# Graph attention on one core: layer 2 with row tiles for five units instead of nine, and a unit's work in another order

## The chip, the cores and the metric

The kernel runs on one core of one Trainium2 chip. Its time is the device time of one execution in microseconds, the median over several runs. The engines are PE (TensorE, matmuls and transposes; its weight loads are listed as PEld), DVE (VectorE), ACT (ScalarE), POOL (GpSimd) and SP (SyncE, which here only issues DMAs). All data are float32 unless said otherwise.

## What is computed

The input is x (8 batches, 2048 nodes, 64 features) and one adjacency matrix of 2048 x 2048 zeros and ones, which all batches share. The densest nodes come first: the chance of a link falls with both node numbers. Cut to what matters:

```python
def _gat_layer(h, mask, b):
    scores = einsum('...nd,...md->...nm', h, h)
    attn = softmax(where(mask, scores, -1e16))
    return einsum('...nm,...md->...nd', attn, h) + b

mask = adj + eye(2048) > 0
h    = einsum('bnc,hdc->bhnd', x, Wh)                  # 4 heads of 64
z    = leaky_relu(cat of _gat_layer(h, mask, bh), 0.2) # layer 1
h2   = einsum('bnk,dk->bnd', z, Wo)                    # 256 -> 64
z2   = leaky_relu(_gat_layer(h2, mask, bo), 0.2)       # layer 2
out  = layernorm(x + layernorm(z2) * gamma + beta)
```

## The kernel before, in words

**Sets and lists.** The first 56 nodes (HUB) have many neighbours and are done densely. The other 1992 are cut into NS = 166 sets of 12. For each set the kernel finds, on the chip, a list of at most 128 nodes that hold all neighbours of the twelve (one column of `index`), and works only with those. One *gather* (`gather`, L797) fetches the rows of such a list: an indirect DMA that POOL issues, 128 rows of 2080 bytes (520 floats: four pairs of batches, each with two columns of ones for the sums), into a *row tile* of 128 partitions.

**Layer 1** works on 83 groups of two sets. Its end writes the rows of the second layer's table (`table2`, L902, issued by SP and at the last by ACT). Near its end the tiles of the first eight blocks of hub work are loaded into the layer-1 row tiles.

**Layer 2** is the place of the change. Its 166 sets make NU = 42 units of four (the last has two). A unit u passes through these steps:
- four gathers into four row tiles (POOL),
- `turn2(u)`: each row tile is transposed by PE in four 128 x 128 pieces (L513), and ACT copies the result out of PSUM into `xts` (L1368; two tiles by one copy of 128 x 1024),
- `scores2(u)`: 32 matmuls of 128 x 128 into the PSUM bank `bank[0]` (L1223), and the exponential by ACT into `eT` (L1226),
- `turn_scores(u)`: four transposes back into the same bank (L1234),
- `keep_scores(u)`: DVE multiplies with the mask `linked` and keeps the weights in `es2` (L1242),
- `values2(u)`: 64 matmuls with the row tiles (L1253), two units into one PSUM tile,
- after every second unit the division by the sums, activation, two layernorms and the residual (`norm`, DVE and ACT), spread over the following units by `work_on(u, 0)` and `work_on(u, 1)`; `roots` (L1326, L1327) takes reciprocal roots on ACT, SP stores the output,
- `spread_own(u)` (L1033, ACT) lays out a unit's own columns, which scores2 needs as weights.

The hub nodes' own attention runs beside this in 19 blocks: `hub_step(k)` makes the scores of block k (L1070, eight matmuls; L1079 DVE, L1082 ACT) and the values of block k-1 (L1093, 16 matmuls). Steps 3 to 8 stand right ahead of layer 2's loop, with scores in `bank[0]`; steps 9 to 19 stand in it, two in the round of u = -3 and one in each after that. Their row tiles `hrows` (six, loaded by SP, `hub_block`, L1059) are filled for blocks 8 to 13 at the start of layer 2 and again inside the loop.

**The order.** Each engine runs its own instructions in the order of the program, and waits on semaphores; nothing reorders them. The loop runs u from -3 and issues, in each round: `turn2(u+3)`, `scores2(u+2)`, a hub step, `values2(u)`, the gathers of unit u+9, `work_on(u, 0)`, `spread_own(u+3)`, `turn_scores(u+1)`, `keep_scores(u+1)`, `work_on(u, 1)`, `roots(u)`. There are 36 row tiles, so the gathers of units 0 to 8 are all issued at the start of layer 2 without a wait between them, and unit u+9 takes the tiles of unit u, each gather waiting for the matmuls of values2 that read its tile. The tiles lie in SBUF in the order of their allocation: first the 36 row tiles, then `xts`, then `hrows`, all in space that layer 1 has used, and what lay there decides what a first write waits for.

Of the kernel before, what the change touches and what calls it, by code (L numbers as in the profile page):

```python
# [30 lines left out]
F32 = mybir.dt.float32  # L31
# [5 lines left out]
OP = mybir.AluOpType  # L37
# [322 lines left out]
def fast_kernel(ctx: ExitStack, tc: tile.TileContext, x, adj, Wh, bh, Wo, bo, gamma, beta, out, flag):  # L360


    nc = tc.nc
    B, N, C = x.shape
# [145 lines left out]
    def turn(tp, rows):  # L510

        for q in range(Q):
            nc.tensor.transpose(tp[:, q * P:(q + 1) * P], rows[:, q, 1:1 + P], ident)  # L513
# [276 lines left out]

    rows = {}
    held = {}

    def gather(table, s, layer, new):
        t = rows[layer, s] = new(f"g{layer}_{s}")
        bound = {} if layer == 2 and s < 36 else dict(bounds_check=N - 1, oob_is_err=False)
        nc.gpsimd.indirect_dma_start(out=t.rearrange("n q c -> n (q c)"), out_offset=None, in_=table,  # L797
                                     in_offset=bass.IndirectOffsetOnAxis(ap=index[:, s:s + 1], axis=0), **bound)

# [253 lines left out]
    def hub_block(k, t):  # L1053
        b = hub_order[k]
        rows["h", k] = t
        n = HUB if b == NHB else hub_sets(b)[1] * SET
        s0 = b * S10
        src = table2[:HUB, :] if b == NHB else table2[HUB:, :].rearrange("(k s) c -> s k c", s=NS)[s0:s0 + n // SET]
        nc.sync.dma_start(out=t.rearrange("n q c -> n (q c)")[:n], in_=src)  # L1059
# [145 lines left out]
    def rows2(name):  # L1205
        return rowt2[int(name[3:]) % 36]

    xts = [late.tile([P, 2, 512], F32, name=f"xts{k}", bufs=1) for k in range(4)]
    hrows = [late.tile([P, Q, PW], F32, name=f"hrows{k}", bufs=1) for k in range(6)]
    for k in range(6):  # L1210
        hub_block(8 + k, hrows[k])
    for u in range(9):
        for s in sets[u]:
            gather(table2, s, 2, rows2)

    def scores2(u):

        w = len(sets[u])
        sp = bank[0].rearrange("p (k n) -> p k n", k=4)
        for k, s in enumerate(sets[u]):  # L1220
            xt = held["T", 2, s // 2].rearrange("c j (q n) -> c j q n", q=Q)
            for q in range(Q):
                nc.tensor.matmul(sp[q * 32:(q + 1) * 32, k, :], bd[u % 3][:, k, q, :], xt[:, s % 2, q, :], start=True, stop=True,  # L1223
                                 tile_position=(0, q * 32))
        e = held["E", u] = late.tile([P, 4, P], F32, tag="eT", name=f"eT{u}", bufs=2)
        nc.scalar.activation(e[:, :w], sp[:, :w], AF.Exp, bias=shifts[:, 1:2], scale=1.0)  # L1226
# [125 lines left out]
    def spread(u, parts):  # L1352

        for k, part in enumerate(parts):
            for t in range(2):
                jobs.setdefault((u + k, t), []).extend(part[t])

    def work_on(u, t):
        for job in jobs.pop((u, t), ()):
            job()  # L1360

    def turn2(u):
        for g in sorted({s // 2 for s in sets[u]}):
# [4 lines left out]
            nc.scalar.copy(t, tp)  # L1368

    tot = late.tile([P, 8], F32, name="tot", bufs=1)  # L1370

# [13 lines left out]
    def in_limits():  # L1385

        nc.vector.tensor_reduce(tot[:, 5:6], tot[:, 0:5], AX.X, OP.min)
        pf = bank2("pf", "T", 2)
        nc.tensor.matmul(pf[0:1, 0, 0:1], tot[:, 5:6], ones, start=True, stop=True)
        fl = late.tile([1, 1], I32, name="fl", bufs=1)  # L1390
        nc.vector.tensor_scalar(fl, pf[0:1, 0, 0:1], P - 0.5, None, OP.is_lt)
        nc.sync.dma_start(out=flag, in_=fl)

    k = 9
    for u in range(-3, NU + 5):
        if u + 3 < NU:
            turn2(u + 3)
        if 0 <= u + 2 < NU:
            scores2(u + 2)
        for _ in range(2 if u == -3 else 1):  # L1400
            if k <= NHB + 1:
                hub_step(k, bank2(f"sh{k}", "T", 2)[:, 0, :] if k <= NHB else None)
                if 8 <= k - 1 and k + 5 <= NHB:
                    hub_block(k + 5, hrows[(k - 1 - 8) % 6])
                if k == NHB + 1:
                    spread(u + 2 - u % 2, norm_hub(u + 2 - u % 2, oh2))
                k += 1
# [9 lines left out]
        work_on(u, 0)  # L1417
        if 3 <= u + 3 < NU:
            spread_own(u + 3)
        if 0 <= u + 1 < NU:  # L1420
            turn_scores(u + 1)
            a = (u + 1) % 2
# [3 lines left out]
            keep_scores(u + 1, a)  # L1426
        work_on(u, 1)
        roots(u)
# [46 lines left out]
```

## Time and profile before

| | |
|---|---|
| time, median of 3 runs | 1018.35 us (1017.01 to 1022.75) |
| span of the profiled execution | 1021.0 us |
| PE busy | 807.8 us (79%) |
| DVE busy | 617.2 us (60%) |
| ACT busy | 521.4 us (51%) |
| POOL busy | 481.3 us (47%) |
| gathers of layer 2, L797 | 166, 1024 ns each, 170.0 us |
| transposes of layer 2, L513 | 664, 280 ns each, 91.6 us |

The profiled execution is one run; its span is 2.65 us above the median. In the page's picture by slices the span is cut into 40 equal parts, and each digit is the busy share of one in tenths. In a timeline a row has its start, its length, engine, line, operation, tiles written and read, the count, and in brackets how long the engine was idle before it and what ended that; "issue" there means that nothing which the profile shows was waited for. Matmuls are pipelined, and their ends are modelled. In the rows by window a window's length is followed by each engine's busy time and count, the granted clock of PE, the share of DMA time and the rate in GB/s.

### The profile page before, as it was taken

The page shows a single profiled execution, that of the slowest core. Times are in us where ns is not written, and L with a number is a line of the kernel's source. Part 1 is how long each engine was busy: PE and PEld are TensorE (multiplying, and loading weights), DVE is VectorE, ACT ScalarE, POOL GpSimd, SP SyncE. Part 2 cuts the span into 40 slices and gives each one's busy share as a digit, 9 for nine tenths or more (in the row PEclk, how much of TensorE's full clock was granted, in tenths as well). Part 3 has the DMA queues.
Part 4 walks back from the last instruction along what each step waited for, and adds up shares of the span by engine and source line. Part 5 has one row for each costly group of instructions (what it writes and reads, how often), then busy time and mean ns, then how long its engine had stood idle before and what let it go on. Part 6 is the DMA issues. An engine that isn't in the chain of part 4 may idle for free.

```text
span 1021.0 us, 42671 instructions
## 1 busy us (share of the span) xinstructions
PE 807.8 (79%) x18437; PEld 685.5 (67%) x18437; DVE 617.2 (60%) x1376; ACT 521.4 (51%) x1042; POOL 481.3 (47%) x614
## 2 busy tenths in 40 slices
PE   3976679899999999999999998419786676667760
PEld 2644457788898888888888887307665555555750
DVE  3449844678777777745555555002267766766795
ACT  2423335556566666666666665005445645555651
POOL 6533214474454555556556630750456556655100
PEclk9989989999999999999999999658999999999985
DMA  8876412453233344444444432764345555445221
GB/s 184 238 208 171 118 44 59 131 134 80 75 91 83 103 124 123 120 124 115 120 119 113 120 86 75 193 184 128 91 112 141 152 147 142 125 134 138 76 53 29
DMA packets 81790, 122.52 MB, mean 120 GB/s; under 512 B 35568, under 2 KB 51852, under 8 KB 81594
## 3 DMA queue, kind: packets, MB, share of 16 engines
q0 software_dynamic: 26784, 65.84, 24.9%
q1 hardware_dynamic: 37702, 49.57, 16.3%
q10 hardware_dynamic: 17108, 4.30, 2.3%
q8 instruction: 147, 2.41, 1.0%
q14 instruction: 49, 0.40, 0.1%
HBM read 123.91 MB, written 18.48 MB: 139 GB/s over the span
## 4 chain that ended last, share of the span: by engine, by line
PE 56%; DVE 13%; issue 9%; ACT 8%; another core or an unknown queue 6%; DMA 4%; POOL 2%; SPq 1%; DVEq 0%; POOLq 0%; ACTq 0%
PE s L826 10%; PE o L851 8%; PE bank L513 7%; PE t L513 6%; PE cat L811 5%; ACT xts L1368 3%; DMA raw<-in_adj_dram 3%; PE cat L532 3%; PE o L868 3%; PE cat L885 3%; PE bank L1234 2%; PE bank L1223 2%; PE cat L895 2%; PE o L1253 2%
## 5 line engine op out<-in xcount | busy, mean ns | idle before, releaser
L797 POOL DMA_INDIRECT g<-table,index x166 | 176.6, 1064 | 207.2 <-PE o L851 165.7
L797 POOL DMA_INDIRECT rows<-table,index x166 | 170.0, 1024 | 147.3 <-PE o L1253 87.5
L831 DVE TENSOR_TENSOR e<-s,mask 128x768 f32<-128x768 f32 x83 | 79.4, 957 | 95.2 <-PE s L826 94.8
L826 PE MATMUL s<-y,xTg 64*64 64x48 f32 x5312 | 115.4, 222 | 5.4 <-issue 3.5
L513 PE MATMUL t<-ident,rows 128*128 128x128 f32 x664 | 91.6, 280 | 31.8 <-issue 30.4
L826 PEld LDWEIGHTS s<-y,xTg 64*64 64x64 f32 x5312 | 98.9, 134 | 25.6 <-issue 20.2
L1368 ACT COPY xts<-t 128x1024 f32<-128x1024 f32 x83 | 79.9, 1011 | 56.2 <-PE t L513 48.5
L513 PEld LDWEIGHTS t<-ident,rows 128*128 128x128 f32 x664 | 76.3, 144 | 40.9 <-issue 39.8
L513 PE MATMUL bank<-ident,g 128*128 128x128 f32 x664 | 100.2, 274 | 0.2 <-ACT otbh L634 0.2
L851 PE MATMUL o<-g,e 128*64 128x65 f32 x2656 | 98.0, 226 | 2.4 <-issue 2.4
L519 ACT ACTIVATE z<-cat,bhp 128x192 f32<-128x192 f32 x166 | 60.7, 417 | 73.9 <-PE cat L532 70.8
L851 PEld LDWEIGHTS o<-g,e 128*64 128x64 f32 x2656 | 85.8, 138 | 12.8 <-issue 3.0
L1129 ACT COPY xTg<-bank 128x512 f32<-128x512 f32 x166 | 89.1, 596 | 0.5 <-PE bank L513 0.3
L1223 PE MATMUL bank<-xts,share 128*32 128x128 f32 x1328 | 56.2, 278 | 34.4 <-issue 19.7
L513 PEld LDWEIGHTS bank<-ident,g 128*128 128x128 f32 x664 | 79.9, 142 | 2.8 <-DVE keysi L766 0.6
L838 ACT ACTIVATE e<-e,shifts 128x768 f32<-128x768 f32 x83 | 80.0, 964 | 2.5 <-DVE e L831 2.5
L817 ACT COPY y<-cat 128x384 f32<-128x384 f32 (+1 forms) x80 | 40.7, 509 | 68.5 <-DVE rowt L899 37.3
L598 ACT ACTIVATE e<-e,shifts 128x896 f32<-128x896 f32 x32 | 33.4, 1043 | 81.4 <-DVE e L595 65.6
L1223 PEld LDWEIGHTS bank<-xts,share 128*32 128x32 f32 x1328 | 38.1, 109 | 50.9 <-issue 44.2
L681 POOL TENSOR_SCALAR a<-raw 120x1024 bf16<-120x1024 int32 (+1 forms) x34 | 38.5, 1135 | 62.1 <-DMA raw<-in_adj_dram 34.7
L811 PE MATMUL cat<-xo,gram 128*128 128x192 f32 (+1 forms) x320 | 65.0, 326 | 0.0
L858 DVE RECIPROCAL rall<-o 64x8 f32<-64x8 f32 x166 | 34.1, 205 | 50.5 <-PE o L851 49.1
(190 smaller groups left out, 1563.0 us busy)
## 6 DMA issues: line engine op xcount, KB each, us to landing
raw<-in_adj_dram SPq DMA_DIRECT2D x32, 480.0 KB
table<-xb SPq DMA_DIRECT2D x22, 256.0 KB
xr_s<-table SPq DMA_DIRECT2D x21, 256.0 KB
table<-x SPq DMA_DIRECT2D x16, 260.0 KB
x<-in_x_dram ACTq DMA_DIRECT2D x32, 128.0 KB
table<-rowt SPq DMA_DIRECT2D x164, 24.4 KB
xb<-in_x_dram SPq DMA_DIRECT2D x164, 24.0 KB
out_dram<-y_s SPq DMA_DIRECT2D x162, 24.0 KB
```

The costliest lines, as they stand in the source:

```text
L513: nc.tensor.transpose(tp[:, q * P:(q + 1) * P], rows[:, q, 1:1 + P], ident)
L519: nc.scalar.activation(z[:, hp], cat[:, :, hp * n:(hp + 1) * n], AF.Identity, bias=bhp[:, hp:hp + 1], scale=1.0)
L797: nc.gpsimd.indirect_dma_start(out=t.rearrange("n q c -> n (q c)"), out_offset=None, in_=table, in_offset=bass.IndirectOffsetOnAxis(ap=ind ...
L811: nc.tensor.matmul(cat[:, k, 2 * GM:2 * GM + n], gram[:, g % 2 * 2 + k, :], held["x", g // 2][:, :n], start=True, stop=True)
L817: nc.scalar.copy(held["y", g // 2][:, :n, g % 2 * 2:g % 2 * 2 + 2], cat[:, :, 2 * GM:2 * GM + n].rearrange("p a n -> p n a"))
L826: nc.tensor.matmul(sp[half(r), p, (q * 2 + j) * M:(q * 2 + j + 1) * M], xt[half(p), j, q, half(r)], y[half(p), (j * Q + q) * M:(j * Q + q ...
L831: nc.vector.tensor_tensor(e[:, :16 * M].rearrange("p (a q n) -> p a q n", a=2, q=Q), sp[:, :, :8 * M].rearrange("p a (q n) -> p a q n", q= ...
L838: nc.scalar.activation(e[:, :16 * M], e[:, :16 * M], AF.Exp, bias=shifts[:, 0:1], scale=1.0)
L851: nc.tensor.matmul(op[half(p), j, o0:o0 + K1], e[:, c0:c0 + 64], rw[j][:, q, sums(p)], start=True, stop=True)
L1129: nc.scalar.copy(t[:, k, :], bank[k])
L1223: nc.tensor.matmul(sp[q * 32:(q + 1) * 32, k, :], bd[u % 3][:, k, q, :], xt[:, s % 2, q, :], start=True, stop=True, tile_position=(0, q * 32))
L1368: nc.scalar.copy(t, tp)
```

## The change

Line numbers behind the change grow by 2 to 9: L797 becomes L799, L1059 L1061, L1223 L1232, L1234 L1243, L1242 L1251, L1253 L1262, L1368 L1377. Five things are different in layer 2; layer 1 is as before.

1. The ring has 20 row tiles (units in flight, LEAD, 5) instead of 36. At the start only the gathers of units 0 and 1 are issued. Those of units 2, 3 and 4 follow in the rounds of u = -3, -2 and -1, each behind a copy of one element on POOL (`seen`) that reads the last tile turned in that round. From u = 0 on, unit u+5 takes the tiles of unit u after values2(u).
2. The four gathers of a unit are issued with the last set first.
3. `xts` and `hrows` are allocated ahead of the row tiles, so they lie elsewhere.
4. A round has another order: values2(u), the gathers of unit u+5, turn_scores(u+1), work_on(u, 0), keep_scores(u+1), a hub step, turn2(u+3), (for u < 0: `seen` and the gathers), scores2(u+2), work_on(u, 1), spread_own(u+3), roots(u).
5. turn2 takes one PSUM bank for each set, with four in flight, and ACT copies 128 x 512 four times a unit instead of 128 x 1024 twice.

```diff
+    LEAD = 5
+    RING = 4 * LEAD
...
-        bound = {} if layer == 2 and s < 36 else dict(bounds_check=N - 1, oob_is_err=False)
+        bound = {} if layer == 2 and s < RING else dict(bounds_check=N - 1, oob_is_err=False)
...
-        nc.vector.tensor_scalar(index[:, :36], index[:, :36], N - 1, None, OP.bitwise_and)
+        nc.vector.tensor_scalar(index[:, :RING], index[:, :RING], N - 1, None, OP.bitwise_and)
...
-    rowt2 = [late.tile([P, Q, PW], F32, name=f"rows2_{k}", bufs=1) for k in range(36)]
...
     xts = [late.tile([P, 2, 512], F32, name=f"xts{k}", bufs=1) for k in range(4)]
     hrows = [late.tile([P, Q, PW], F32, name=f"hrows{k}", bufs=1) for k in range(6)]
+    rowt2 = [late.tile([P, Q, PW], F32, name=f"rows2_{k}", bufs=1) for k in range(RING)]
+    seen = late.tile([1, 1], F32, name="seen", bufs=1)
...
+    def gathers(u):
+        for s in sets[u][-1:] + sets[u][:-1]:
+            gather(table2, s, 2, rows2)
+
     for k in range(6):
         hub_block(8 + k, hrows[k])
-    for u in range(9):
-        for s in sets[u]:
-            gather(table2, s, 2, rows2)
+    for u in range(2):
+        gathers(u)
...
     def turn2(u):
-        for g in sorted({s // 2 for s in sets[u]}):
-            tp = bank2(f"t2_{g}", "T", 2)
-            for j in range(2):
-                turn(tp[:, j, :], rows[2, 2 * g + j])
-            t = held["T", 2, g] = xts[g % 4]
-            nc.scalar.copy(t, tp)
+        for s in sets[u]:
+            if s % 2 == 0:
+                held["T", 2, s // 2] = xts[s // 2 % 4]
+            tp = bank1(f"t2_{s}")
+            turn(tp, rows[2, s])
+            nc.scalar.copy(xts[s // 2 % 4][:, s % 2, :], tp)
...
     for u in range(-3, NU + 5):
-        if u + 3 < NU:
-            turn2(u + 3)
-        if 0 <= u + 2 < NU:
-            scores2(u + 2)
-        for _ in range(2 if u == -3 else 1):
...
             values2(op, sets[u], es2[a], a, len(sets[u + 1]) if a == 0 else 0)
             if a == 1:
                 spread(u, norm_sets(u // 2, op))
-        for s in sets[u + 9] if 0 <= u < NU - 9 else []:
-            gather(table2, s, 2, rows2)
+            if u + LEAD < NU:
+                gathers(u + LEAD)
+        if 0 <= u + 1 < NU:
+            turn_scores(u + 1)
         work_on(u, 0)
+        if 0 <= u + 1 < NU:
...
+            keep_scores(u + 1, a)
+        for _ in range(2 if u == -3 else 1):
...
+        if u + 3 < NU:
+            turn2(u + 3)
+        if u < 0:
+            nc.gpsimd.tensor_copy(seen, held["T", 2, sets[u + 3][-1] // 2][0:1, 1, 0:1])
+            gathers(u + LEAD)
+        if 0 <= u + 2 < NU:
+            scores2(u + 2)
+        work_on(u, 1)
         if 3 <= u + 3 < NU:
             spread_own(u + 3)
```

What that does to the engines is shown at three places. The rows give line, operation, the tile written, the tiles read, and in brackets the semaphores waited for, by the engine or DMA queue that signals them; `rows_k` is a row tile, `table` the table of layer 2. First POOL at the start of layer 2, before: the first gathers of the 36.

```order
L797 DMA rows_0_11559<-table_99,index 128x520 [waits DMAHW3_49,DMAHW4_49,DMAHW2_49,DMAHW5_49,DMAHW1_49,DMAHW6_49,DMAHW0_49,DMAHW7_49,DMASW3_49,PE_49]
L797 DMA rows_1_11560<-table_99,index 128x520 [waits DVE_49,DMASW4_49,Activation_49,Pool_49]
L797 DMA rows_2_11561<-table_99,index 128x520 [waits DMASW5_49]
L797 DMA rows_3_11562<-table_99,index 128x520 [waits DMASW6_49]
L797 DMA rows_4_11563<-table_99,index 128x520 [waits DMASW7_49]
L797 DMA rows_5_11564<-table_99,index 128x520 [waits DMASW0_49]
```

The same place now, from the seventh gather on:

```order
L799 DMA rows_5_11574<-table_99,index 128x520 [waits DMASW1_49]
L799 DMA rows_6_11575<-table_99,index 128x520 [waits DMASW2_49]
L1434 COPY seen<-xts_11560 1x1 [waits Activation_49]
L799 DMA rows_11_11580<-table_99,index 128x520 [waits DMASW3_49]
L799 DMA rows_8_11577<-table_99,index 128x520 [waits DMASW4_49]
L799 DMA rows_9_11578<-table_99,index 128x520 [waits DMASW5_49]
L799 DMA rows_10_11579<-table_99,index 128x520 [waits DMASW6_49]
L1434 COPY seen<-xts_11562 1x1 [waits Activation_49,Pool_49]
```

After eight gathers stands a copy that waits for ACT, then four gathers, then the next copy; before, none of the following ones waited for a compute engine.

The second place is POOL in the loop, before: unit 9 takes the tiles of unit 0, unit 10 those of unit 1.

```order
L797 DMA rows_0_11559<-table_99,index 128x520 [waits DMASW7_49,PE_49]
L797 DMA rows_1_11560<-table_99,index 128x520 [waits DMASW0_49,PE_49]
L797 DMA rows_2_11561<-table_99,index 128x520 [waits DMASW1_49,PE_49]
L797 DMA rows_3_11562<-table_99,index 128x520 [waits DMASW2_49,PE_49]
L797 DMA rows_4_11563<-table_99,index 128x520 [waits DMASW3_49,PE_49]
```

And now, unit 5 in the tiles of unit 0 and unit 6 in those of unit 1:

```order
L799 DMA rows_3_11572<-table_99,index 128x520 [waits DMASW7_49,PE_49]
L799 DMA rows_0_11569<-table_99,index 128x520 [waits DMASW0_49]
L799 DMA rows_1_11570<-table_99,index 128x520 [waits DMASW1_49]
L799 DMA rows_2_11571<-table_99,index 128x520 [waits DMASW2_49]
L799 DMA rows_7_11576<-table_99,index 128x520 [waits DMASW3_49,PE_49]
```

Each of four gathers waited for PE; now the first does, for the last set of values2, and the other three only for their DMA lane.

The third place is SP at the start of layer 2, before: the last store into the table of layer 2, and the loads of hub tiles.

```order
L902 DMA table_99<-rowt_114 4x12x130 [waits DMAHW0_49,DVE_49]
L1059 DMA hrows_11599<-table_99 120x1x520 [waits DMAHW5_49,DMAHW1_49,PE_49]
L1059 DMA hrows_11600<-table_99 120x1x520 [waits DMAHW2_49]
L1059 DMA hrows_11601<-table_99 120x1x520 [waits DMAHW3_49]
L1059 DMA hrows_11602<-table_99 120x1x520 [waits DMAHW4_49]
```

And now:

```order
L904 DMA table_99<-rowt_114 4x12x130 [waits DMAHW0_49,DVE_49]
L1061 DMA hrows_11563<-table_99 120x1x520 [waits DMAHW1_49,Activation_49,Pool_49]
L1061 DMA hrows_11564<-table_99 120x1x520 [waits DMAHW2_49]
L1061 DMA hrows_11565<-table_99 120x1x520 [waits DMAHW3_49]
L1061 DMA hrows_11566<-table_99 120x1x520 [waits DMAHW4_49]
```

The first load waited for PE, namely for the hub values of block 7 (L1093), which read a tile that lay in the same space; now it waits for ACT and POOL, for work that belongs to layer 1, and not for PE.

More of the change, by code (lines that the diff above doesn't have):

```diff
@@ L1201, in bank2, with bank1, rows2 @@
         return psum2.tile([P, 2, 512], F32, tag=tag, name=name, bufs=bufs)
-    rowt2 = [late.tile([P, Q, PW], F32, name=f"rows2_{k}", bufs=1) for k in range(36)]
-    def rows2(name):
-        return rowt2[int(name[3:]) % 36]
     xts = [late.tile([P, 2, 512], F32, name=f"xts{k}", bufs=1) for k in range(4)]
     hrows = [late.tile([P, Q, PW], F32, name=f"hrows{k}", bufs=1) for k in range(6)]
+    rowt2 = [late.tile([P, Q, PW], F32, name=f"rows2_{k}", bufs=1) for k in range(RING)]
+    seen = late.tile([1, 1], F32, name="seen", bufs=1)
+    def bank1(name):
+        return psum2.tile([P, 512], F32, tag="T", name=name, bufs=4)
+    def rows2(name):
+        return rowt2[int(name[3:]) % RING]
+    def gathers(u):
+        for s in sets[u][-1:] + sets[u][:-1]:
+            gather(table2, s, 2, rows2)
     for k in range(6):
         hub_block(8 + k, hrows[k])
-    for u in range(9):
-        for s in sets[u]:
-            gather(table2, s, 2, rows2)
+    for u in range(2):
+        gathers(u)
     def scores2(u):
@@ L1387, in in_limits @@
         nc.vector.tensor_reduce(tot[:, 5:6], tot[:, 0:5], AX.X, OP.min)
-        pf = bank2("pf", "T", 2)
-        nc.tensor.matmul(pf[0:1, 0, 0:1], tot[:, 5:6], ones, start=True, stop=True)
+        pf = bank1("pf")
+        nc.tensor.matmul(pf[0:1, 0:1], tot[:, 5:6], ones, start=True, stop=True)
         fl = late.tile([1, 1], I32, name="fl", bufs=1)
-        nc.vector.tensor_scalar(fl, pf[0:1, 0, 0:1], P - 0.5, None, OP.is_lt)
+        nc.vector.tensor_scalar(fl, pf[0:1, 0:1], P - 0.5, None, OP.is_lt)
         nc.sync.dma_start(out=flag, in_=fl)
@@ L1395, in fast_kernel @@
     for u in range(-3, NU + 5):
-        if u + 3 < NU:
-            turn2(u + 3)
-        if 0 <= u + 2 < NU:
-            scores2(u + 2)
-        for _ in range(2 if u == -3 else 1):
[L1401 to L1407, printed above, removed]
         if 0 <= u < NU:
@@ L1414, in fast_kernel @@
                 spread(u, norm_sets(u // 2, op))
-        for s in sets[u + 9] if 0 <= u < NU - 9 else []:
-            gather(table2, s, 2, rows2)
-        work_on(u, 0)
-        if 3 <= u + 3 < NU:
-            spread_own(u + 3)
+            if u + LEAD < NU:
+                gathers(u + LEAD)
         if 0 <= u + 1 < NU:
             turn_scores(u + 1)
+        work_on(u, 0)
+        if 0 <= u + 1 < NU:
             a = (u + 1) % 2
@@ L1426, in fast_kernel @@
             keep_scores(u + 1, a)
+        for _ in range(2 if u == -3 else 1):
+            if k <= NHB + 1:
+                hub_step(k, bank1(f"sh{k}") if k <= NHB else None)
+                if 8 <= k - 1 and k + 5 <= NHB:
+                    hub_block(k + 5, hrows[(k - 1 - 8) % 6])
+                if k == NHB + 1:
+                    spread(u + 2 - u % 2, norm_hub(u + 2 - u % 2, oh2))
+                k += 1
+        if u + 3 < NU:
[5 more added lines that the diff above has]
+            scores2(u + 2)
         work_on(u, 1)
+        if 3 <= u + 3 < NU:
+            spread_own(u + 3)
         roots(u)
```

## The prediction

> **What bounds the kernel now.** I read the page first, then the chain of waits between 620 and 730 us, the timeline around its longest piece, SP's waits, and last the windows and groups of layer 2. The page says that no engine is full over the whole span, and that PE collapses in the middle of it:
>
> ```profile
> span 1021.0 us, 42671 instructions
> PE   3976679899999999999999998419786676667760
> POOL 6533214474454555556556630750456556655100
> ```
>
> A digit is 25.5 us. PE's 26th and 27th are 4 and 1, at 638 to 689 us, where POOL's are 7 and 5: here layer 2 begins. The chain of waits shows what the end of the kernel hangs on there:
>
> ```profile
> 636.05 53.60 another core or an unknown queue
> 689.65 3.67 DMA hrows<-table
> 693.46 1.14 PE bank L1093 x16
> ...
> 697.53 2.25 PE t L513 x16
> 699.78 1.01 PE bank L1223 x32
> ...
> 702.43 1.90 PE t L513 x16
> ...
> 711.96 1.04 PE o L1253 x64
> ...
> 720.57 1.04 PE o L1253 x64
> ```
>
> The chain has no name for 53.60 us. SP's waits have the same length at the load of a hub tile, which suits one wait on PE, and the timeline shows what POOL and PE do meanwhile:
>
> ```profile
> SPq L1059 <- remote: 53.8, 1, 53.8
> ```
>
> ```profile
> 638.71 0.98 POOL L797 DMA_INDIRECT rows<-table,index  x1 [4.47 <-ACT share L1082]
> 639.99 0.96 POOL L797 DMA_INDIRECT rows<-table,index  x1 [0.30 <-issue]
> ...
> 641.94 1.09 PE L1070 MATMUL bank<-share,own 128*120 128x112 f32 x8 [0.72 <-issue]
> ...
> 648.12 1.94 PE L1070 MATMUL bank<-share,own 128*120 128x112 f32 x8 [4.48 <-DVE share L1079]
> ...
> 682.52 0.95 POOL L797 DMA_INDIRECT rows<-table,index  x1 [0.30 <-issue]
> ...
> 687.42 0.37 PE L513 MATMUL t<-ident,rows 128*128 128x128 f32 x1 [1.03 <-issue]
> ```
>
> ```profile
> 660.00:680.00 20.00, 3.18 (x9) 1.65 (x9) 0.00 (x0) 0.00 (x0) 15.13 (x16) 0.50 0.75 211
> ```
>
> POOL issues 36 gathers back to back (638.71 to 682.52: 1.25 us each). PE runs nine transposes in 20 us, waiting for nothing but "issue", DVE and ACT run nothing. The gate opens when the gathers stop: 16 transposes that trickled until 687.42 take 2.25 us at 697.53. So a train of gathers holds PE, and the hub load (which waits for PE to have read an older tile) comes after it.
>
> The units behind this, cut at the starts of values2 of units 0, 6, 32, 36 and 41 and the end (time, PE, PEld, DVE, ACT, POOL, clock, DMA):
>
> ```profile
> 711.90:764.30 52.40, 41.39 (x804) 33.47 (x802) 21.18 (x40) 23.18 (x40) 24.91 (x24) 0.93 0.37 97
> 764.30:948.10 183.80, 128.57 (x3018) 107.49 (x3021) 125.47 (x223) 103.26 (x189) 108.71 (x104) 1.00 0.52 140
> 948.10:971.50 23.40, 19.25 (x472) 17.58 (x475) 18.94 (x34) 16.55 (x30) 2.25 (x2) 0.93 0.26 65
> 971.50:993.90 22.40, 14.68 (x454) 12.82 (x442) 20.64 (x39) 11.34 (x24) 0.00 (x0) 0.88 0.21 50
> 993.90:1021.00 27.10, 1.28 (x34) 0.94 (x34) 15.69 (x31) 3.88 (x10) 1.20 (x2) 0.50 0.15 34
> ```
>
> The second row has 104 gathers, four for each of 26 units: 183.80/26 = 7.07 us a unit, with no engine at 75%. The fourth row has none: 22.40/5 = 4.48 us, with DVE at 92%. Gathers cost a unit some 2.6 us, and one unit's timeline shows how:
>
> ```profile
> 855.72 1.13 PE L1253 MATMUL o<-rows,share 128*32 128x65 f32 x62
> ...
> 856.44 1.00 POOL L797 DMA_INDIRECT rows<-table,index  x1 [1.55 <-PE o L1253]
> ...
> 857.75 1.01 POOL L797 DMA_INDIRECT rows<-table,index  x1 [0.30 <-issue]
> ...
> 859.55 1.00 POOL L797 DMA_INDIRECT rows<-table,index  x1 [0.79 <-PE bank L1234]
> ...
> 860.53 0.55 DVE L1242 TENSOR_TENSOR share<-bank,maskh 128x384 f32<-128x384 f32 x1
> ...
> 860.85 1.00 POOL L797 DMA_INDIRECT rows<-table,index  x1 [0.30 <-issue]
> ...
> 862.45 0.47 PE L1223 MATMUL bank<-xts,share 128*32 128x128 f32 x8 [0.32 <-issue]
> ...
> 863.42 1.06 POOL L797 DMA_INDIRECT rows<-table,index  x1 [1.57 <-PE o L1253]
> ```
>
> The third gather waits only for the third set of values2, which PE had run by 856.85, and starts 0.79 us after the second ends. So what PE has finished is seen late by others while gathers run, and soon once they pause: the third gather starts 0.79 us after the pause began, of which 0.30 is POOL's own, and the scores go on at 862.45, 0.60 after the fourth ended. I take 0.55 us for that.
>
> **The start of layer 2.** Eight gathers go at once instead of 36: 28 x 1.25 = 35.0 us less of the train, so PE is free near 651 us. The hub tiles no longer lie where a tile lay that PE still reads; they are issued near 636 us, and the path from issue to first use, 693.46 - 689.65 = 3.8 us, lies beside the short train. The 53.8 us of SP's wait are not a gain of their own: they are the same stall. Three trains of four are added, one in each round ahead of unit 0, each behind a copy of one element on POOL. That copy waits for ACT's copy of the last tile turned. Behind it on POOL stand only the gathers, whose tiles PE wants two rounds later, so its own time is hidden. What a train costs the round is the question. A round without gathers took 702.43 - 697.53 = 4.9 us; one with gathers and values2 took 720.57 - 711.96 = 8.6, so 8.6 - 4.9 - 1.04 = 2.7 us a train, 8 us for three. Bounds: nothing, if PE's own work covers it, and 3 x 5.2 = 15.6 if all is serial. Gain: 35.0 + 3.8 - 8.0 = 30.8 us (23.2 to 38.8). Units 0 to 5, with four gathers and hub steps in each as before, keep their 52.4 us, so unit 6 starts at 764.3 - 30.8 = 733.5.
>
> A rule of the notes speaks to this. The Trainium skill, "SBUF — State Buffer", section "Who interferes with whom", says that DMA never contends with a compute engine and that "PE and ACT never wait on anyone." Nine transposes in 20 us with no wait but "issue" speak against it, so the trace decides; what the rule would make of the time is the third rival.
>
> **A unit in steady state.** On PE nothing changes place in the cycle: values2, turned scores, transposes, scores, values2 again. The gathers now wait once, for the last set of values2, and run as one train of four. Three terms against 7.07:
> - the pause of 0.79 us ahead of the third falls to the 0.30 of issue: -0.49.
> - the first waits for four sets instead of one: three quarters of 1.13 us, +0.85.
> - turned scores and transposes come to PE with the whole train ahead of them, so that the rest of the scores, 0.47 us in the row at 862.45, may be done when it ends: -0.47 at best, and I take most of it, since 24 of 32 were done inside the shorter train.
>
> That is 6.96 to 7.43; I take 7.0. The bounds lie further out, because one train of four is not shown. If PE does the scores and half of values2 inside the train, the unit is the train, 0.55, the other half, 0.5, and 0.3 for POOL to start: 4 x 1.31 - 0.30 = 4.94, and 6.3 in all. If turned scores pass late and the scores wait for the train's end, it is 4.94 + 0.55 + 1.01 (scores) + 1.04 (values2), from the chain's rows, + 0.3 = 7.85.
>
> The 512-wide copies of ACT are dearer:
>
> ```profile
> L1368 ACT COPY xts<-t 128x1024 f32<-128x1024 f32 x83 | 79.9, 1011 | 56.2 <-PE t L513 48.5
> L1129 ACT COPY xTg<-bank 128x512 f32<-128x512 f32 x166 | 89.1, 596 | 0.5 <-PE bank L513 0.3
> ```
>
> 4 x 0.596 - 2 x 1.011 = +0.36 us a unit, on an engine that is busy 103.26 of 183.80 us; the scores that follow use the round before's copies, so it costs nothing unless ACT is late, and then 0.36 x 41 = 15 us. The hub steps of units 0 to 5 come ahead of the transposes of their round, not behind the scores: the same instructions, beside the same gathers. spread_own (ACT) moves behind the scores' exponentials and is wanted a round later, and one DVE operation on the lists covers 20 columns, not 36: nothing for both.
>
> **The sum.** Units up to 36 now carry gathers, not up to 32: 30 x 7.0 = 210 us from unit 6 to 36, against 183.80 + 23.40 = 207.2. So 733.5 + 210 = 943.5; five units without gathers, +22.4 = 965.9; the tail, +27.1 = 993.0 (these two, 49.5 us, stand in every case). The profiled span, 1021.0, lies 2.65 over the median of 1018.35, which is taken off: **990 us**.
>
> **Rivals.**
> - *The train of four holds PE to its end.* For: the train of 36 did, and turned scores got through before only after the pause between two and two, which is gone now (the copy from them, L1242, ran at 860.53, behind the third gather's start). Against: transposes did trickle. Then the chain behind the train is 0.55 + 0.55 (L1242) + 1.01 + 1.04 + 0.3 and a unit takes 4.94 + 3.45 = 8.4 us: 733.5 + 252 + 49.5 - 2.65 = 1032, slower. It turns slower than before from (1021.0 - 49.5 - 733.5)/30 = 7.93 us a unit. Chance 0.18.
> - *POOL alone sets the pace.* If PE's work is seen at once, 5.24 + 0.3 = 5.5 us: 733.5 + 165 + 49.5 - 2.65 = 945. For: four gathers without a wait between them. Against: every train so far delayed PE. Chance 0.12.
> - *The stall at the start is not made by the gathers* but by whatever else lies at 640 to 690 us; then only the hub load's 3.8 us go: 764.3 - 3.8 + 210 + 49.5 - 2.65 = 1017, no change. For: PE's idle time is put down to "issue", not to POOL. Against: PE runs freely within 5 us of the last gather. The rule quoted above belongs to this case. Chance 0.07.
>
> **How the numbers follow.** The forecast's own case has 0.63. Its bounds are 961 (38.8 and 6.3: 725.5 + 189 + 49.5 - 2.65) and 1023 (23.2 and 7.85: 741.1 + 235.5 + 49.5 - 2.65). 0.5% is 5 us, about what a measurement of this kernel can tell from no change: faster is below 1013, slower above 1023. Faster: 0.58 of the forecast's 0.63 and the 0.12 of the second rival, 0.70. Same: 0.05 of the forecast and the 0.07, 0.12. Slower: 0.18. The range leaves out about a tenth on each side: 958 lies just under the forecast's low end and leaves out most of the second rival, and 1030 reaches into the first, whose price would have to come out in full to pass it.
>
> **What would show it.** Right: the slices at 640 to 690 us stay at 6 or more on PE, SP's wait at the hub load is gone from the head of its list, values2 of unit 0 starts near 681 us and of unit 6 near 733, and unit 6 to 36 takes 7.0 us each, with POOL's third gather idle 0.30. Wrong: values2 of unit 0 still near 710 (third rival); units of 8 us and more, with L1242 starting after the fourth gather (first); units under 6, POOL busy 80% and more (second).

## The result and the profile after

The changed kernel takes 1007.89 us (median of 4 runs, 1004.59 to 1009.34), the kernel before in the same comparison 1020.55 us (4 runs, 1017.01 to 1024.62): a ratio of 0.988, interval 0.984 to 0.992. It is faster by 1.2%, 12.7 us, where 28 were forecast. The chips of the later experiments are of two kinds, on which the same kernels take quite different times (before: 1020 us on the one, 889 us on the other); each ratio below is to the kernel before on the same chip. The changed kernel itself was run on the chip of the first measurement and on one later chip, so some comparisons with it are between two chips of one kind, and say so.

The profiled execution has a span of 1005.2 us, 15.8 less than before. First the page's slices, PE, POOL and PE's clock:

```profile
span 1005.2 us, 42772 instructions
PE   3876688899999999999999998667777787777660
POOL 6533233474454565655556650335455555565500
PEclk9999989999999999999999999788998889999975
```

The hole is gone: where PE had 4 and 1 it has 6 and 6. The timeline at the start of layer 2 shows the last of the eight gathers, the hub step that waited for it, and the paced trains:

```profile
635.20 0.98 POOL L799 DMA_INDIRECT rows<-table,index  x1 [4.73 <-DMA hrows<-table]
...
644.01 0.95 POOL L799 DMA_INDIRECT rows<-table,index  x1 [0.30 <-issue]
646.12 0.62 DVE L1081 TENSOR_TENSOR share<-bank,maskt 120x448 f32<-120x448 f32 x1 [7.64 <-remote]
...
657.06 0.18 POOL L1434 COPY seen<-xts 1x1 f32<-1x1 f32 x1 [12.09 <-ACT xts L1377]
...
675.84 1.09 PE L1262 MATMUL o<-rows,share 128*32 128x65 f32 x64
```

PE's part of the hub step is seen at 646.12, 1.2 us behind the end of the train of eight; before, PE was held until 687. SP's longest wait at a load of hub tiles is 15.4 us, not 53.8:

```profile
SPq L1061 <- PE bank L1095: 15.4, 1, 15.4
```

values2 of unit 0 starts at 675.8, 40.6 us behind the first gather; before it was 711.9 - 638.7 = 73.2.

The windows are cut at the same points as before: values2 of units 0, 6, 36 and 41, and the end.

```profile
675.80:729.20 53.40, 41.23 (x836) 35.65 (x832) 21.17 (x39) 25.13 (x53) 28.75 (x29) 0.90 0.47 130
729.20:950.10 220.90, 162.82 (x3495) 144.64 (x3488) 141.61 (x256) 127.82 (x276) 125.05 (x120) 0.91 0.50 135
950.10:978.30 28.20, 20.06 (x498) 18.10 (x490) 21.22 (x39) 14.83 (x33) 2.00 (x2) 0.80 0.24 59
978.30:1005.20 26.90, 1.28 (x34) 0.93 (x34) 15.71 (x31) 3.90 (x10) 1.21 (x2) 0.50 0.15 35
```

The 30 units from 6 to 36 took 207.20 us before and now 220.90, 7.36 each; the last five 22.40 and now 28.20, though they have no gathers. So the start gives some 32 us and the units take back 19.5. One pair of units shows a wait that was not there:

```profile
856.11 0.69 ACT L1235 ACTIVATE eT<-bank,shifts 128x512 f32<-128x512 f32 x1 [2.44 <-remote]
856.70 0.70 ACT L1035 COPY share<-own 64x192 f32<-64x192 f32 x2
...
857.42 0.31 ACT L1335 ACTIVATE var<-var,shifts 128x16 f32<-128x16 f32 x1
857.76 0.22 ACT L1336 ACTIVATE var<-var 128x16 f32<-128x16 f32 x1
...
858.01 0.69 DVE L1314 TENSOR_TENSOR y_s<-y_s,var 128x512 f32<-128x512 f32 x1 [5.47 <-ACT var L1336]
...
860.52 0.69 DVE L1285 TENSOR_TENSOR y_s<-o,rall 128x512 f32<-128x512 f32 x1
861.13 0.55 DVE L1251 TENSOR_TENSOR share<-bank,maskh 128x384 f32<-128x384 f32 x1
...
861.82 1.08 PE L1232 MATMUL bank<-xts,share 128*32 128x128 f32 x32 [2.55 <-DVE share L1251]
...
864.21 1.00 POOL L799 DMA_INDIRECT rows<-table,index  x1 [1.88 <-PE o L1262]
```

ACT takes the exponential (L1235) and spread_own (L1035) ahead of the roots (L1335, L1336). DVE stands 5.47 us for these, then does six operations of the norm, and keep_scores (L1251) behind them; PE stands 2.55 us for keep_scores, and only then come the scores, values2 and the next train. The groups of the stretch with 104 gathers say how often, first before, then now (busy, mean, idle time and what ended it):

```profile
L1305 DVE TENSOR_TENSOR y_s<-y_s,var 128x512 f32<-128x512 f32 x26 | 17.9, 690 | 7.1 <-ACT var L1327 7.1
```

```profile
L1232 PE MATMUL bank<-xts,share 128*32 128x128 f32 x843 | 32.3, 291 | 27.3 <-DVE share L1251 25.1 <-ACT xts L1377 0.9 <-DVE y_h L1285 0.9
L1314 DVE TENSOR_TENSOR y_s<-y_s,var 128x512 f32<-128x512 f32 x26 | 17.8, 686 | 62.5 <-ACT var L1336 55.0 <-ACT var L1335 7.5
```

DVE's wait for the roots grew from 7.1 to 62.5 us, and 25.1 us of PE's idle time end with keep_scores. The reason lies in the order of the program; the experiments below test it. ACT's roots(u) used to stand ahead of the exponential that follows keep_scores(u+1) by way of the scores; now they stand behind it, and behind spread_own. keep_scores, scores, exponential, spread_own, roots, DVE's norm, keep_scores: every second unit goes once round this chain.

### The profile page after: what moved, and what is told of

The parts are those of the page before. It is cut to its first block, busy times and chain, and to the rows that moved or that the text cites. A ratio compares the mean times of both kernels' runs of the same rounds, so it can differ in the third digit from the quotient of the medians.

```text
span 1005.2 us, 42772 instructions
## 1 busy us (share of the span) xinstructions
PE 815.8 (81%) x18437; PEld 706.5 (70%) x18437; DVE 613.5 (61%) x1376; ACT 532.1 (53%) x1125; POOL 483.2 (48%) x617
## 3 DMA queue, kind: packets, MB, share of 16 engines
q0 software_dynamic: 26784, 64.88, 24.6%
## 4 chain that ended last, share of the span: by engine, by line
PE 55%; DVE 15%; ACT 10%; issue 9%; another core or an unknown queue 5%; DMA 3%; POOL 3%; DVEq 0%; POOLq 0%; ACTq 0%
PE s L828 10%; PE o L853 8%; PE bank L513 7%; PE cat L813 5%; PE cat L532 3%; PE o L870 3%; PE bank L1232 3%; PE t L513 3%; PE cat L887 3%; ACT xts L1377 2%; PE o L1262 2%; DMA raw<-in_adj_dram 2%; PE cat L897 2%; ACT eT L1235 2%
## 5 line engine op out<-in xcount | busy, mean ns | idle before, releaser
L799 POOL DMA_INDIRECT g<-table,index x166 | 176.5, 1064 | 202.6 <-PE o L853 160.7
L799 POOL DMA_INDIRECT rows<-table,index x166 | 170.9, 1029 | 131.3 <-PE o L1262 85.3
L828 PEld LDWEIGHTS s<-y,xTg 64*64 64x64 f32 x5312 | 99.0, 134 | 24.3 <-issue 19.5
L519 ACT ACTIVATE z<-cat,bhp 128x192 f32<-128x192 f32 x166 | 60.8, 417 | 72.0 <-PE cat L532 71.9
L1377 ACT COPY xts<-t 128x512 f32<-128x512 f32 x166 | 87.1, 593 | 21.6 <-PE t L513 17.8
L1262 PE MATMUL o<-rows,share 128*32 128x65 f32 x2656 | 70.9, 247 | 26.4 <-issue 25.6
L513 PE MATMUL t<-ident,rows 128*128 128x128 f32 x664 | 87.4, 287 | 5.0 <-issue 3.2
L1232 PE MATMUL bank<-xts,share 128*32 128x128 f32 x1328 | 53.8, 295 | 44.3 <-DVE share L1251 38.8
L513 PEld LDWEIGHTS t<-ident,rows 128*128 128x128 f32 x664 | 80.6, 150 | 6.6 <-issue 3.8
L1262 PEld LDWEIGHTS o<-rows,share 128*32 128x32 f32 x2656 | 60.6, 127 | 35.0 <-issue 33.8
L1314 DVE TENSOR_TENSOR y_s<-y_s,var 128x512 f32<-128x512 f32 x42 | 28.9, 687 | 89.2 <-ACT var L1336 81.8
L1232 PEld LDWEIGHTS bank<-xts,share 128*32 128x32 f32 x1328 | 39.9, 116 | 54.2 <-issue 38.9
```

The source lines that it names most:

```text
L519: nc.scalar.activation(z[:, hp], cat[:, :, hp * n:(hp + 1) * n], AF.Identity, bias=bhp[:, hp:hp + 1], scale=1.0)
L828: nc.tensor.matmul(sp[half(r), p, (q * 2 + j) * M:(q * 2 + j + 1) * M], xt[half(p), j, q, half(r)], y[half(p), (j * Q + q) * M:(j * Q + q ...
L1262: nc.tensor.matmul(op[t * 32:(t + 1) * 32, f, k * W2 + p:k * W2 + p + K1], e[:, 2 * q + p, k, :], rw[:, q, sums(p)], start=(a == 0 and k = ...
L1377: nc.scalar.copy(xts[s // 2 % 4][:, s % 2, :], tp)
```

## The experiments

Two theories. The **order theory**: the place of the roots costs what is missing. The **train theory**: the uninterrupted train of four gathers does.

### The roots put back (three runs)

```diff
             keep_scores(u + 1, a)
+        work_on(u, 1)
+        roots(u)
         for _ in range(2 if u == -3 else 1):
...
             scores2(u + 2)
-        work_on(u, 1)
         if 3 <= u + 3 < NU:
             spread_own(u + 3)
-        roots(u)
```

> The changed kernel with work_on(u, 1) and roots(u) put back right behind keep_scores(u+1), ahead of the hub step, the transposes and the scores; everything else as changed. The order theory: in the changed round the roots of ACT stand behind the exponential of scores2(u+2), DVE waits for them ahead of keep_scores of the next unit (5.2 us idle at L1314 in every second unit), PE idles 2.6 us and its clock falls to 0.56 now and then. It expects some 10 us less between units 6 and 36 (7.39 to about 7.05 us a unit) and 5 us less in the last five: about 993 us, clock near 1.0 in that stretch. The train theory (four gathers without a pause are what costs the units): no change, 1004 to 1010 us.

Measured: 888.96 us against 888.52 before, ratio 1.000 (0.997 to 1.004). All times were far below the expected ones: this chip runs the kernel before in 889 us. So the kernels were run again together, the changed one and the one before among them:

> The changed kernel as it is, on whichever chip this falls. The runs so far fall into two kinds: in the first, a train of gathers held back what PE had finished, and the kernel before took 1020 us; in the second, PE runs freely beside the same train, and it takes 888 us. If this chip holds PE: 1005 to 1010 us against 1018 to 1023, as first measured. If it does not, the start has nothing to win and the wait for the roots remains: slower than before, 915 to 925 against 888.

Measured: 923.59 us, ratio 1.040 (1.034 to 1.046).

> The kernel before, as it is, for its profile on this chip. If PE is held: a stall of some 50 us at the start of layer 2 and units of 7.0 us. If not: no stall, values2 of unit 0 some 30 us behind the first gather, and units of 5 us on the mean, 10 for each pair.

Measured: 891.9 us in one run. Its window over the first 29 gathers, and one place in it:

```profile
616.00:651.00 35.00, 30.80 (x463) 27.45 (x464) 8.69 (x17) 17.48 (x24) 26.47 (x29) 0.95 0.87 260
```

```profile
638.35 0.95 POOL L797 DMA_INDIRECT rows<-table,index  x1 [0.30 <-issue]
638.39 1.73 PEld L513 LDWEIGHTS t<-ident,rows 128*128 128x128 f32 x16
638.39 1.97 PE L513 MATMUL t<-ident,rows 128*128 128x128 f32 x16
```

The same train of 36, in the same pitch, and PE is busy 30.80 of 35 us beside it: sixteen transposes in 1.97 us, where the first profile had nine in 20. The stall is not there on this chip. From the first gather to unit 6 the kernel before takes 684.4 - 615.8 = 68.6 us and the changed one 676.6 - 611.2 = 65.4: the start gives 3.2 us, where it gave 31.6 in the first measurement. Units 6 to 36 take 191.3 us against 155.8, and the change is 4% slower.

> The changed kernel with work_on(u, 1) and roots(u) back behind keep_scores, as in the first experiment. If this chip holds PE: the order theory expects 990 to 996 us against 1020 before; the train theory 1004 to 1010. If it does not: 885 to 892, as measured.

Measured: 890.06 us, ratio 1.002 (0.999 to 1.006), on the chip of the 923.59. The roots, with the work_on(u, 1) that moved along with them, are worth 33.5 us there. The time is that of the kernel before, but two differences cancel in it. Up to unit 6 it takes 674.7 - 613.9 = 60.8 us, 7.8 less; units 6 to 36 take 164.9 us against 155.8, 9.1 more. In them PE's transposes wait longer for gathers to land (nearly all of these units, first before, then now):

```profile
L513 PE MATMUL t<-ident,rows 128*128 128x128 f32 x480 | 59.4, 273 | 3.2 <-DMA rows<-table,index 2.9
```

```profile
L513 PE MATMUL t<-ident,rows 128*128 128x128 f32 x475 | 61.9, 277 | 14.6 <-DMA rows<-table,index 14.5
```

So the rest of the change is not free in the loop of this chip. That the ring of five units makes the gathers late was not tested here.

Last, on a chip that holds PE (before: 1019.26 us):

> The changed kernel with work_on(u, 1) and roots(u) back behind keep_scores, sent once more for a chip where a train of gathers holds PE. There the order theory expects 990 to 996 us against 1020 before and 1008 as changed, the train theory 1004 to 1010. Where PE is free: 885 to 892.

Measured: 999.31 us, ratio 0.982 (0.978 to 0.987), beside 0.988 (0.984 to 0.992) as changed. The changed kernel was not run beside it; against its 1007.89 us of the first measurement it is 8.6 us better, and the two intervals overlap slightly. The trace is plainer. Its windows (units 6 to 36, the last five) and groups, units 6 to 32:

```profile
731.00:944.60 213.60, 167.12 (x3509) 142.47 (x3502) 144.27 (x255) 125.35 (x278) 123.02 (x120) 0.94 0.51 141
944.60:970.00 25.40, 16.89 (x474) 15.11 (x462) 18.84 (x35) 14.49 (x33) 2.00 (x2) 0.93 0.22 59
```

```profile
L1232 PE MATMUL bank<-xts,share 128*32 128x128 f32 x833 | 28.4, 276 | 0.0
L1314 DVE TENSOR_TENSOR y_s<-y_s,var 128x512 f32<-128x512 f32 x26 | 18.5, 712 | 7.7 <-ACT var L1336 5.3 <-ACT var L1335 2.5
```

DVE's wait is back at 7.7 us and PE's for keep_scores is nil; units 6 to 36 are 7.3 us shorter than in the first measurement of the changed kernel, the last five 2.8. (Unit 36 is cut where the bulk of its values2 runs; ten of its matmuls pass beside the last train from 941.4 on, so the sum of the two, 10.1, is firmer than its parts.) The order theory expected 990 to 996 here: its sign holds, its size was 3 to 9 us too large.

### The roots moved in the kernel before

```diff
             scores2(u + 2)
+        work_on(u - 1, 1)
+        roots(u - 1)
...
-        work_on(u, 1)
-        roots(u)
```

The loop runs one round longer for the last of them.

> The kernel before, with one thing of the change: work_on(u, 1) and roots(u) stand behind the next round's scores2, so that ACT takes the roots after the scores' exponential. Everything else as before (36 tiles, all at once, old order). The order theory: DVE waits for the roots ahead of the next keep_scores, as in the changed kernel less spread_own's 0.7 us in every second unit; slower than before by 8 to 20 us on a chip where PE is free (897 to 909 against 889), by some 5 to 10 where it is held. If the changed kernel's slower units come from the ring or the trains, nothing changes.

Measured: 921.83 us against 888.63, ratio 1.039 (1.034 to 1.044): on a chip that leaves PE free, with this edit alone, the kernel before becomes as slow as the changed one (923.59 on the other chip of this kind). That is more than the 8 to 20 expected; beside DVE's wait PE now waits too:

```profile
L1223 PE MATMUL bank<-xts,share 128*32 128x128 f32 x960 | 32.4, 275 | 38.8 <-DVE share L1242 25.4 <-ACT share L1033 13.4
L1305 DVE TENSOR_TENSOR y_s<-y_s,var 128x512 f32<-128x512 f32 x30 | 20.6, 688 | 38.6 <-ACT var L1327 38.6
```

spread_own (L1033), which now comes behind the late roots on ACT, is late for the next scores; I had not counted that.

### Spread_own behind the roots

```diff
         work_on(u, 1)
+        roots(u)
         if 3 <= u + 3 < NU:
             spread_own(u + 3)
-        roots(u)
```

> The changed kernel with spread_own(u+3) behind roots(u) instead of ahead of it; nothing else. The order theory: the chain keep_scores, scores2, exponential, spread_own, roots, DVE's next jobs, keep_scores loses spread_own's 0.70 us in every second unit, 20 times: 14 us less than the changed kernel, about 909 on a chip where PE is free and about 1000 where it is held. If the wait for the roots is not what sets the pace: no change.

Measured: 902.87 us, ratio 1.015 (1.009 to 1.020), beside 1.040 as changed (on the other chip of this kind): 21 us for 0.70 us taken out of the chain in every second unit. Here work_on(u, 1) stays where it is, so ACT's order alone does this: the chain sets the pace. Its own part was put at 14 us. For the other 7 the clock may account, which this run does not separate: PE's mean clock rose from 0.949 to 0.975, and the scores' matmuls fell from 304 to 275 ns each.

### Each gather waiting for its own set

```diff
-        for s in sets[u][-1:] + sets[u][:-1]:
+        for s in sets[u]:
```

> The changed kernel with a unit's gathers issued from the first set to the last, so that each waits for its own set's matmuls as before. The train theory expects the pause between gathers back and the first gather 0.85 us earlier in a unit: 7.0 us a unit, 8 to 10 us less in all, about 998 us. The order theory expects at most 3 us of change, 1005 to 1010, since the wait for the roots stays.

Measured: 922.97 us, ratio 1.039 (1.036 to 1.043), the same as changed, on a chip that leaves PE free. The wait for the roots is still there and sets the pace, so a gain from the pause could be hidden behind it. On a chip that holds PE this was not tried; there the trains of four with the roots put back gave 213.60/30 = 7.12 us a unit, against 7.07 with two pauses before. That leaves the train theory at most what lies between 7.12 and the 7.0 that were forecast: 3.6 of the 10.9 us that are missing from unit 6 to 36.

### The old order, with five and with six units in the ring

The round in the order of before; ring, pacing, hub tiles and transposes as changed.

```diff
     for u in range(-3, NU + 5):
+        if u + 3 < NU:
+            turn2(u + 3)
...
+        if 0 <= u + 2 < NU:
+            scores2(u + 2)
...
             if u + LEAD < NU:
                 gathers(u + LEAD)
+        work_on(u, 0)
+        if 3 <= u + 3 < NU:
+            spread_own(u + 3)
         if 0 <= u + 1 < NU:
             turn_scores(u + 1)
...
             keep_scores(u + 1, a)
-        for _ in range(2 if u == -3 else 1):
...
         work_on(u, 1)
-        if 3 <= u + 3 < NU:
-            spread_own(u + 3)
         roots(u)
```

> The changed kernel with the round written in the order of before (transposes, scores, hub step, values2, gathers of unit u+5, work_on(u, 0), spread_own, turned scores, keep_scores, work_on(u, 1), roots); ring of 20, pacing, moved hub tiles, copies of 512 and trains of four stay. The order theory expects what it does for the roots put back: 990 to 996 us, 4.5 us a unit in the last five. The train theory expects 1004 to 1010, with units of 7.3 us or more while gathers run.

Measured: 923.36 us, ratio 1.040 (1.034 to 1.046): a miss for the order theory at first sight. The transposes' groups tell why (690 to 830 us):

```profile
L513 PE MATMUL t<-ident,rows 128*128 128x128 f32 x374 | 53.9, 284 | 25.3 <-DMA rows<-table,index 24.8 <-PE t L513 0.2
```

In the old order a tile is transposed one unit earlier, so a ring of five leaves the gathers too little time to land: 24.8 us of waits for them, against 7.0 in the same stretch with the roots put back on this chip. DVE's wait for the roots is small here, 6.5 us, so this is another wait. With one unit more:

```diff
-    LEAD = 5
+    LEAD = 6
...
-    for u in range(2):
+    for u in range(3):
         gathers(u)
```

> The old order of the round with tiles for six units instead of five (three units' gathers at once, the rest paced), hub tiles moved, transposes one set a bank. In the run with five units and the old order PE waited 24.8 us for gathers to land between 690 and 830 us. If that was all that made it 923 us, six units give the time of before, 886 to 894 where PE is free. Where PE is held: the stall at the start gone and units of 7.0 us, 990 to 998 against 1020. If the ring itself costs something else, 905 and more where PE is free.

Measured, on the chip that holds PE: 998.03 us, ratio 0.978 (0.972 to 0.985), with 7.07 us a unit:

```profile
738.00:950.00 212.00, 164.40 (x3479) 141.80 (x3471) 141.22 (x248) 122.78 (x277) 120.49 (x118) 0.94 0.51 139
```

This is the time of the roots put back, within the intervals. It is faster than the kernel before on a chip that holds PE; beside the changed kernel's 0.988 of the first measurement the intervals just meet. On a chip that does not hold PE it was not tried, so that the late landing was all that made the 923 us is not settled.

### Three smaller pieces

Only the hub tiles moved, in the kernel before:

```diff
-    rowt2 = [late.tile([P, Q, PW], F32, name=f"rows2_{k}", bufs=1) for k in range(36)]
...
     hrows = [late.tile([P, Q, PW], F32, name=f"hrows{k}", bufs=1) for k in range(6)]
+    rowt2 = [late.tile([P, Q, PW], F32, name=f"rows2_{k}", bufs=1) for k in range(36)]
```

> The kernel before, with only xts and hrows allocated ahead of the 36 row tiles; all 36 gathers still at once, order as before. If the train of gathers makes the stall at the start, the wait of SP goes and the stall stays: values2 of unit 0 still near 708 to 712 us, time 1015 to 1020 us. If the wait for the hub tile makes it, values2 of unit 0 comes some 30 us earlier and the time falls to about 990.

Measured: 888.35 us, ratio 1.001 (0.998 to 1.004). This chip has no stall to remove, so the run says only that the move costs nothing there; the two causes of the stall it could not tell apart.

All 20 gathers at once:

```diff
-    for u in range(2):
+    for u in range(LEAD):
         gathers(u)
...
-        if u < 0:
-            nc.gpsimd.tensor_copy(seen, held["T", 2, sets[u + 3][-1] // 2][0:1, 1, 0:1])
-            gathers(u + LEAD)
```

> The changed kernel with the first 20 gathers at once and no copies of one element; order and ring as changed. Where PE is held by a train: 12 x 1.25 = 15 us more of it at the start, less about 8 for the three paced trains, so some 7 us slower than the changed kernel. Where PE is free: between 4 us faster (POOL starts unit 4's train 6 us earlier) and no change, 918 to 924.

Measured: 924.85 us, ratio 1.040 (1.034 to 1.046), on a chip that leaves PE free: beside the changed kernel's 923.59 on the other chip of this kind the pacing costs nothing, and what it gains where PE is held was not tried alone.

The roots put back and no bounds check:

```diff
-        bound = {} if layer == 2 and s < RING else dict(bounds_check=N - 1, oob_is_err=False)
+        bound = {} if layer == 2 else dict(bounds_check=N - 1, oob_is_err=False)
...
-        nc.vector.tensor_scalar(index[:, :RING], index[:, :RING], N - 1, None, OP.bitwise_and)
+        nc.vector.tensor_scalar(index, index, N - 1, None, OP.bitwise_and)
```

> The changed kernel with work_on(u, 1) and roots(u) back behind keep_scores, and all gathers without a bounds check (the lists are masked for all 166 sets, so empty places fetch some row whose weight is zero; the output is the same). Where PE is free, the gathers' own length sets the pace: 0.95 instead of 1.00 us each for 146 of them, 7 us less, 880 to 885 against 889. Where PE is held: 985 to 996 by the order theory, 1000 to 1010 by the train theory.

Measured: 895.57 us, ratio 1.008 (1.005 to 1.010): slower, not faster, than the kernel before, and 6.6 us slower than the first run of the roots put back on this chip. POOL's queue moves 76.75 MB instead of 64.88, since empty places now fetch rows, and a gather is hardly shorter (1089 ns between 685 and 841 us, against 1102 in that run).

## Why the prediction was wrong

- **The start** was right: from the first gather to unit 6 it took 764.3 - 638.7 = 125.6 us and takes 729.2 - 635.2 = 94.0, 31.6 less against 30.8 forecast. That the length of the train makes the stall is read from the profiles: PE is free 1.2 us behind eight gathers, some 4 us behind 36, and in the old order with six units, which sends twelve at once, DVE sees PE's work at 659.80, 2.6 us behind the last of them. No run changed the train alone on a chip that holds PE.
- **The unit with a train of four**, 7.0 us, was right as a number for the gathers: 7.12 and 7.07 on the chip that holds PE, once the roots are out of the way. The scores do run beside the train, as its third term supposed: from 852.37 to 853.46, in a train that ends at 855.14. The first rival (8.4 us) did not come.
- **The step that failed** is the one on a unit's other work: "spread_own (ACT) moves behind the scores' exponentials and is wanted a round later ... nothing". It looked at when spread_own's result is wanted, and at PE's order, and never at what stands behind it on ACT: roots(u), which had moved behind the exponential too, and for which DVE waits ahead of keep_scores. Units 6 to 36 took 220.9 us, not 210 (+10.9), the last five 28.2, not 22.4 (+5.8). Putting the roots back took 7.3 and 2.8 us of that away. The cause of the rest, 3.6 and 3.0, stays open. The old order with six units leaves 2.0 from unit 6 to 36 (212.0) and 0.6 in the last five (23.0, from 950.0 to 973.0), so the new order, with the roots put back, still has a part in the last five: PE waits 2.9 us there for keep_scores. Both runs also have a lower clock from unit 6 to 36, 0.94, than the kernel before (0.99).
- **From span to time**: 2.65 us were taken off for a profiled run above the median. The profiled run now took 1007.0 us for a span of 1005.2, near its median of 1007.89: 5.3 us of the miss are this. Layer 1 ended 3.5 us earlier than in the profile before, without a change there; that is luck, for in the two later traces of this kind the first gather of layer 2 starts at 637.6 and 642.4, not at 635.2. The start gave 0.8 more than forecast, and the tail was 0.2 shorter. Together 990.3 - 3.5 - 0.8 + 10.9 + 5.8 - 0.2 + 5.3 = 1007.8.
- **The third rival** is not the explanation here. On a chip that leaves PE free its premise holds, that gathers do not hold PE, but there is no stall either, and the change is slower there by about what the roots cost.

## What to carry to other kernels

When a round is written in another order, follow the chain on every engine's queue, not only the bounding one's: list for each instruction that moves what now stands ahead of it in its own queue, and who waits for it. A small operation (two of 0.3 and 0.2 us here) put behind one that hangs on the other end of the loop closes a cycle, and the cycle sets the pace. And a gain that rests on a disturbance between engines is worth measuring on more than one chip.

## What the runs showed of the hardware

The unexpected thing is the two kinds of chips. On the one, trains of gathers hold back PE's finished work: 1012 to 1025 us for the kernel before, and in the loop of the changed kernel values2 passes some four matmuls in 0.7 us until the train ends:

```profile
853.78 0.31 PE L1262 MATMUL o<-rows,share 128*32 128x65 f32 x4 [0.29 <-issue]
854.14 1.00 POOL L799 DMA_INDIRECT rows<-table,index  x1 [0.30 <-issue]
854.49 0.34 PE L1262 MATMUL o<-rows,share 128*32 128x65 f32 x5 [0.40 <-issue]
...
855.93 1.00 PE L1262 MATMUL o<-rows,share 128*32 128x65 f32 x53 [0.50 <-issue]
```

On the other (two chips), the same program takes 881 to 896 us, and sixteen transposes pass beside a train in 1.97 us. The Trainium skill's "PE and ACT never wait on anyone" ("SBUF — State Buffer", section "Who interferes with whom") agrees with the second kind and not with the first. What makes the difference stays open. One of the free chips was met twice, 26 minutes apart, and was free both times; PE was held in the first measurement and in one later session, so that it belongs to the chip, and not to the occasion, is likely but not shown. One difference goes with it, and its meaning is open too: the first kind's traces hold 8,471 to 8,943 DMA semaphore events each, the second kind's 12,065 to 12,267, for the same transfers.

The other is PE's clock. In the unit at 846 us of the changed kernel, behind a wait for keep_scores of 2.55 us, it is 0.56:

```profile
841.90:846.40 4.50, 2.07 (x19) 1.83 (x17) 3.58 (x8) 2.77 (x7) 3.58 (x4) 1.00 0.34 94
846.40:850.00 3.60, 3.48 (x97) 3.33 (x98) 3.50 (x6) 1.72 (x4) 0.63 (x1) 0.56 0.57 145
857.00:862.00 5.00, 2.45 (x28) 2.24 (x32) 3.87 (x8) 2.96 (x8) 3.88 (x4) 1.00 0.36 90
```

The scores and values2 there take 1.68 and 2.04 us, against 1.08 and 1.24 in the unit at 861. But that unit too had sixteen transposes and then a wait of 2.55 us ahead of its scores (third row, as far as the scores' start), and its clock stayed at 1.00. The trace's record of the clock tells them apart. It changes in steps of 3.41 us: a step at half clock runs from 846.85 to 850.27, and in the step ahead of it PE is busy for 0.86 us, 25%. The wait at 861 falls into two steps, with PE busy for 2.18 and 2.10 us. From 735 to 950 us, 11 of 62 steps are at half clock; in the steps just ahead of them PE is busy 22 to 57% of the time, ahead of the others 50% or more. Transposes count in this: from 915.12 to 918.53 PE ran nothing else, for 1.70 us, and the next step has the full clock. The Trainium skill ("TensorE: Matmul & The Clock Gate", section "Part 4: PE-mode transpose") says that a transpose does not count as PE being busy in the same way; this trace does not bear that out. A wait that looks harmless can so cost the work behind it as well, depending on where it falls.
